# Loading the relative destinations and attribute rows of a graph network four chunks at a time

## The chip, the cores and the metric

The kernel runs on one core of a Trainium2 chip. The metric is the device time of one execution in microseconds. Before the change it is 8192.53 us, the median of three runs (8170.84, 8192.53, 8251.86). The engines are named as the profile names them: PE (TensorE; PEld is its weight load), DVE (VectorE), ACT (ScalarE), POOL (GpSimd) and SP (SyncE, which here only issues transfers).

## What is computed

A graph with 6,250 nodes of 128 features and 200,000 edges sorted by destination goes through two message-passing convolutions and one attention layer. Only the part that runs over the edges matters here. Cut to it, the reference is:

```python
def mesh_conv(x, src, dst, ea, w1, b1, g, bt, w2, b2):
    m = jnp.concatenate([x[dst], x[src], ea], axis=-1) @ w1 + b1
    m = jax.nn.silu(group_norm(m, g, bt))
    m = m @ w2 + b2
    out = jax.ops.segment_sum(m, dst, num_segments=n)
    cnt = jax.ops.segment_sum(jnp.ones((dst.shape[0],), m.dtype), dst, num_segments=n)
    return out / jnp.clip(cnt, 1.0)[:, None]
...
logits = (q[dst] * k[src]).sum(-1) * scale + (edge_attr @ ew + eb)
amax = jax.ops.segment_max(logits, dst, num_segments=n)
pe = jnp.exp(logits - amax[dst])
ssum = jax.ops.segment_sum(pe, dst, num_segments=n)
w = pe / jnp.clip(ssum[dst], 1e-06)
o = jax.ops.segment_sum(w[:, :, None] * v[src], dst, num_segments=n)
```

## The kernel before

The edges are cut into 196 chunks (`NCH`) of 1,024 edges (`CH`): 8 tiles (`NT`) of 128. Three stages run over all chunks, one after another: the first convolution, the second, and attention. Between them stand short node stages, which project all nodes and write tables to memory: `a_d` (the part of x[dst] @ w1, three bf16 pieces of a row of 128) and `b_d` (the part of x[src] @ w1) for the convolutions, `a_d` and `kv_d` for attention.

A chunk's destinations lie in a window of 112 (`WN`) rows of the table, because the edges are sorted. So x[dst] is not gathered: a one-hot matrix picks the rows by matmul. `rel_d` holds each edge's destination relative to its chunk's window, one row of 128 for each tile. `loads` (L442) does for one chunk: it spreads the chunk's 1,024 relative destinations over 112 partitions with one transfer into the tile `rel_b` (L447, 224 KB); it loads 16 (`KE`) rows of attributes and constants into partitions 112 to 127 of the tile `ohT` (L450, 32 KB); it loads the window's 112 table rows into one of three fixed tiles `pk` (L453, 84 KB); and on DVE it compares `rel_b` with the partition's number, which gives the one-hot matrix in partitions 0 to 111 of `ohT` (L454). The tile `ohT` is then the stationary side of 24 matmuls with `pk` (L578 in the convolutions, L740 in attention, where L746 uses it once more), which give the edge's destination part and its attribute part in one product.

`gather` (L457) fetches the source part: 8 indirect transfers from POOL for each chunk (L459), into one of 13 tiles `g` in a convolution, 11 in attention. In a convolution DVE adds the two parts (L590), ACT squares them (L592), DVE reduces the squares (L593). After a group of 8 chunks (`G`) ACT takes the square root of the group's variances; then each chunk gets its normalisation on DVE (L604, L607, L608), silu on ACT (L609), a one-hot matrix of its edges' destinations in the 128-row window on DVE (L465), its segment sum by 8 matmuls (L614), two masked copies on ACT (L648) and the addition into the table on DVE (L639). Attention has the same shape: products with the keys (L752), their reduction (L754), a segmented maximum for each group of 8 with rows `nbs` and `nbe` loaded from SP (L786), then weights and sums (L828).

`pipeline` (L524) sets the program order: in turn it starts chunk n+1 (`ahead`: loads, gather, products), does the first step of chunk n, and the second step of one or two chunks of the group before. The framework's scheduler moves instructions within each engine's queue somewhat from there; each engine then works its queue strictly in order, and so does SP with its transfers. Tiles come from pools with a fixed number of buffers: a tile is written again only when all that used its earlier content have finished. `rel` has 3 buffers in a convolution and 2 in attention, `ohT` has 3, `pk` are 3 tiles, and the PSUM tile `m` of the products has 2. So the transfers and the comparison for chunk c wait for the matmuls of chunk c-3.

Of the kernel before, what the change touches and what calls it, by code (L numbers as in the profile page):

```python
# [9 lines left out]
BF = mybir.dt.bfloat16  # L10
I32 = mybir.dt.int32
AF = mybir.ActivationFunctionType
ALU = mybir.AluOpType
# [6 lines left out]
P = 128  # L20
# [3 lines left out]
NT = 8  # L24
CH = NT * P
G = 8
WN = 112
KE = P - WN
PITCH = D + 4
# [8 lines left out]
def kernel(ctx: ExitStack, tc: tile.TileContext, x, src, dst, eat, w, out):  # L38
# [10 lines left out]
    nc = tc.nc  # L49
    N = x.shape[0]  # L50
    EW = src.shape[1]
    NCH = EW // NT
# [18 lines left out]
    iota_p = const.tile([P, 1], FP, name="iota_p")  # L71
# [39 lines left out]
    with tc.tile_pool(name="wprep", bufs=2) as wp:  # L111
# [18 lines left out]
        for i in (1, 2):  # L130
            t = const.tile([P, 2 * D], FP, name=f"wab_{i}")
# [4 lines left out]
            t = wp.tile([5, D], FP, name="wcb")  # L136
# [4 lines left out]
        t = wp.tile([5, H], FP, name="web")  # L141
# [24 lines left out]
    nc.vector.memset(web3, 0.0)  # L166
    nc.sync.dma_start(out=web3[WN:P, :], in_=web3_d)

# [14 lines left out]
    rel_d = dram.tile([EW, P], BF, name="rel_d")  # L183
    nbs_d = dram.tile([EW, P], BF, name="nbs_d")
    nbe_d = dram.tile([EW, P], BF, name="nbe_d")
    ea_d = dram.tile([KE, E], BF, name="ea_d")
    with tc.tile_pool(name="prep", bufs=1) as pp, tc.tile_pool(name="rows", bufs=2) as rp, \
            tc.tile_pool(name="prep_ps", bufs=2, space=PSUM) as pps:
        def by_chunk(t):
            return t.rearrange("p (c t) -> p c t", t=NT)  # L190
# [53 lines left out]
        rel = pp.tile([P, EW], FP, name="rel")  # L244
# [3 lines left out]
        nc.vector.scalar_tensor_tensor(  # L248
            by_chunk(main), by_chunk(rel), float(WN), good[:, :, None].to_broadcast([P, NCH, NT]),
            ALU.is_lt, ALU.mult)  # L250
# [66 lines left out]
        for a in range(4):  # L317
            t = rp.tile([P, EW], FP, name="ea_f")
# [115 lines left out]
    def value(t, c, engine, top):  # L434
        return nc.values_load(t[0:1, c:c + 1] if isinstance(c, int) else t[0:1, bass.ds(c, 1)],
                              engines=[engine], min_val=0, max_val=top,
                              skip_runtime_bounds_check_because=WHY)

    class Chunk:
        pass  # L440

    def loads(c, pools, rows_d):  # L442
        k = Chunk()
        k.c = c
        k.src, k.dm = src_i[:, c * NT:(c + 1) * NT], dm0[:, c * NT:(c + 1) * NT]
        k.rel = pools["rel"].tile([WN, CH], BF, name="rel_b")
        nc.sync.dma_start(  # L447
            out=k.rel, in_=rel_d[c * NT:(c + 1) * NT, :].rearrange("t p -> (t p)")[None, :].to_broadcast([WN, CH]))
        k.ohT = pools["ohT"].tile([P, CH], BF, name="ohT")
        nc.sync.dma_start(out=k.ohT[WN:P, :], in_=ea_d[:, c * CH:(c + 1) * CH])  # L450
        k.pk = pk[c % NPK]
        first = value(lo_i, c, SP, N - 1)
        nc.sync.dma_start(out=k.pk[:WN].rearrange("p s c -> p (s c)"), in_=rows_d[bass.ds(first, WN), :])  # L453
        nc.vector.tensor_scalar(k.ohT[:WN, :], k.rel, iota_p[:WN], None, ALU.is_equal)  # L454
        return k

    def gather(k, g, table_d):  # L457
# [56 lines left out]
    def spread(n):  # L514

        sizes = [G] * max(0, (n - 5) // G)
        rest = n - sum(sizes)
        while rest:
            s = min(max(rest // 2, 1), G)
            sizes.append(s)  # L520
# [26 lines left out]
    def conv(i):  # L547
# [3 lines left out]
        wide = D + 1 if i == 1 else D  # L551
        with ExitStack() as es:
            pool = lambda n, b, **kw: es.enter_context(tc.tile_pool(name=f"{n}{i}", bufs=b, **kw))
            pools = {"rel": pool("rel", 3), "ohT": pool("ohT", 3), "oh": pool("oh", 3),
                     "ps": pool("ps", 1, space=PSUM), "left": pool("left", 1)}
            gp, wk, vp = pool("gp", 1), pool("wk", 2), pool("vp", 2)
            ps_ = pools["ps"]

            gs = [gp.tile([P, NT, PITCH], FP, name=f"g{j}") for j in range(G + 5)]
            if i == 1:  # L560
# [19 lines left out]
            def ahead(c):  # L580
                k = loads(c, pools, a3_d[i])
                k.g = gs[c % len(gs)]
                gather(k, k.g, b_d[i])
                hidden(k, [(k.ohT, k.pk)])
                return k

            def first(k, var, j):

                k.mt = k.g[:, :, :D]
                nc.vector.tensor_tensor(k.mt, k.m, k.mt, ALU.add)  # L590
                sq = wk.tile([P, NT, D], FP, name="sq")
                nc.scalar.activation(sq, k.mt, AF.Square)  # L592
                return lambda: nc.vector.tensor_reduce(  # L593
                    var[:, j * NT * H:(j + 1) * NT * H], sq.rearrange("p t (g c) -> p (t g) c", c=HD), AX.X, ALU.add)

            def deviations(n, var):
                sd = vp.tile([P, G * NT * H], FP, name="sd")
                nc.scalar.activation(sd[:, :n], var[:, :n], AF.Sqrt, bias=eps_t, scale=1.0 / HD)
                rs = ps_.tile([P, G * NT * H], FP, name="rs")
                nc.vector.reciprocal(rs[:, :n], sd[:, :n])  # L600
                return rs
# [17 lines left out]
            def first_step(k):  # L619
                for f in state["reduce"]:  # L620
                    f()
                if state["j"] == 0:
                    state["var"] = vp.tile([P, G * NT * H], FP, name="var")
                state["reduce"] = [first(k, state["var"], state["j"])]
# [47 lines left out]
    def after_conv(i, A):  # L672
# [15 lines left out]
        nc.scalar.activation(A[:, :NW, :], A[:, :NW, :], AF.Silu)  # L688

    conv(1)  # L690
    with tc.tile_pool(name="node1", bufs=1) as np_:
        A = np_.tile([P, NW + 1, D], FP, name="A")
        after_conv(1, A)
        nc.vector.tensor_tensor(A[:, :NW, :], A[:, :NW, :], temb[:, None, :].to_broadcast([P, NW, D]), ALU.add)
        make_ab(A, 2)
    conv(2)
    with tc.tile_pool(name="node2", bufs=1) as np_:
        A = np_.tile([P, NW + 1, D], FP, name="A")
# [24 lines left out]
        nc.sync.dma_start(out=t[WN:P].rearrange("p s c -> p (s c)"), in_=zeros_b[:KE, :])  # L723
    with ExitStack() as es:
        pool = lambda n, b, **kw: es.enter_context(tc.tile_pool(name=f"{n}a", bufs=b, **kw))
        pools = {"rel": pool("rel", 2), "ohT": pool("ohT", 3), "oh": pool("oh", 2),
                 "ps": pool("ps", 1, space=PSUM)}
        gp, wk = pool("gp", G + 3), pool("wk", 2)
        ps_ = pools["ps"]
# [30 lines left out]
        def ahead(c):  # L760
            k = loads(c, pools, a3_d[3])
            k.g = gp.tile([P, NT, KV], FP, name="g")
            gather(k, k.g, kv_d)
            k.qe = []
            products(k, k.ohT, k.pk)
            biases(k, k.ohT, web3)
            return k
# [232 lines left out]
```

## Time and profile before

| | |
|---|---|
| median of three runs | 8192.53 us (8170.84 to 8251.86) |
| the profiled execution | 8242.21 us, its span 8240.4 us |
| mean granted TensorE clock | 0.666 |
| DMA | 702.81 MB, mean 85 GB/s, 422,049 packets |
| queue of SP's and ACT's transfers q1 | 210,920 packets, 258.43 MB, 10.3% of 16 engines |
| POOL's gathers q0 | 175,616 packets, 417.77 MB, 18.7% of 16 engines |
| the comparison L454 | 588 times, 299.1 us busy, median 480 ns |
| the gathers L459 | 4,704 of 0.95 to 0.97 us |

The page of the profile shows one execution. Its first part is each engine's busy time; the second is the span in 40 slices, where the two convolutions fill slices 2 to 27 and attention the rest; a further part lists groups of instructions by line, with the time the engine sat idle before them and what ended that time. "issue" means that the engine waited for nothing that the profile shows, "remote" that a semaphore ended the wait and the profile can't name who set it. Times in the timelines are microseconds from the start of the span. The chain of waits that ended last covers only the last node stage in this trace, so the edge stages have to be read from the waits and the timelines.

### The profile page before, as it was taken

What the parts mean: (1) busy time and instruction counts of PE and PEld (TensorE: products, weight loads), DVE (VectorE), ACT (ScalarE), POOL (GpSimd) and SP (SyncE); (2) the same over time, 40 slices, a digit from 0 to 9 for tenths busy, and PEclk for the clock granted to TensorE, in tenths of its full rate; (3) what the DMA queues carried; (4) which work ended last, traced back from release to release, by engine and by line L of the source; (5) the groups of instructions that cost most, each with busy time, mean ns of one, the idle gap of its engine ahead of it and who ended that gap; (6) DMA issues with size and microseconds to landing.
All of it is one profiled execution on the core that took longest, in us unless ns stands there. A gap on an engine that the chain in (4) does not pass through costs nothing. (4 is left out here: it accounts for less than half of the span.)

```text
span 8240.4 us, 87011 instructions
## 1 busy us (share of the span) xinstructions
PE 3684.0 (45%) x26465; PEld 3255.2 (40%) x26466; DVE 5153.9 (63%) x7719; ACT 1631.0 (20%) x3110; POOL 4542.3 (55%) x4723
## 2 busy tenths in 40 slices
PE   2144444444444414444444444442555555555553
PEld 1133343334334313433334433332444545544542
DVE  5266666666666726666666666683666666666666
ACT  2122222222222312222222222230000000000001
POOL 2556566666565056656656665504666666666650
PEclk9566666666666656666666666676676666666666
DMA  5222222222222122222222222213444444444441
GB/s 160 63 70 71 69 74 73 71 72 73 68 70 65 43 61 73 70 68 72 72 70 71 73 73 69 65 71 111 118 120 120 120 120 120 120 120 118 120 110 48
DMA packets 422049, 702.81 MB, mean 85 GB/s; under 512 B 116780, under 2 KB 237444, under 8 KB 421060
## 3 DMA queue, kind: packets, MB, share of 16 engines
q0 software_dynamic: 175616, 417.77, 18.7%
q1 hardware_dynamic: 210920, 258.43, 10.3%
q10 hardware_dynamic: 35036, 20.95, 0.9%
q8 instruction: 215, 3.52, 0.2%
q14 instruction: 262, 2.15, 0.1%
HBM read 649.99 MB, written 46.67 MB: 85 GB/s over the span
## 5 line engine op out<-in xcount | busy, mean ns | idle before, releaser
L459 POOL DMA_INDIRECT g<-b_d,src_i x3136 | 2977.0, 949 | 2227.8 <-PE u L614 785.5
L459 POOL DMA_INDIRECT g<-kv_d,src_i x1568 | 1523.4, 972 | 1164.6 <-issue 418.7
L614 PE MATMUL u<-g,oh 128*128 128x129 f32 (+1 forms) x6272 | 1292.0, 380 | 1309.6 <-ACT g L609 659.9
L614 PEld LDWEIGHTS u<-g,oh 128*128 128x128 f32 x6272 | 1183.8, 286 | 1418.7 <-ACT g L609 710.8
L578 PE MATMUL m<-pk,ohT 128*128 128x128 bf16 x9408 | 894.5, 258 | 1609.9 <-issue 977.8
L578 PEld LDWEIGHTS <-ohT 128*128 128x128 bf16 x9408 | 744.8, 118 | 1742.4 <-issue 1170.7
L639 DVE TENSOR_TENSOR flat<-flat,u 128x258 f32 (+1 forms) x392 | 164.2, 419 | 1343.2 <-ACT u L648 1178.1
L828 PE MATMUL u<-g,oh 128*128 128x145 f32 x3136 | 785.8, 438 | 420.6 <-issue 361.7
L828 PEld LDWEIGHTS u<-g,oh 128*128 128x128 f32 x3136 | 723.7, 318 | 454.8 <-issue 391.0
L648 ACT ACTIVATE u<-u,mask 128x129 f32<-128x129 f32 (+1 forms) x784 | 266.5, 340 | 2152.5 <-remote 1250.7
L590 DVE TENSOR_TENSOR g<-m,g 128x1024 f32<-128x1024 f32 x392 | 476.2, 1215 | 290.8 <-remote 232.8
L740 PE MATMUL qe<-pk,ohT 128*128 128x128 bf16 x4704 | 439.1, 257 | 367.0 <-DVE g L752 226.3
L609 ACT ACTIVATE g<-g 128x1024 f32<-128x1024 f32 x392 | 414.1, 1056 | 925.8 <-DVE g L608 471.4
L592 ACT ACTIVATE sq<-g 128x1024 f32<-128x1024 f32 x392 | 414.3, 1057 | 718.6 <-DVE g L590 438.7
L740 PEld LDWEIGHTS <-ohT 128*128 128x128 bf16 x4704 | 382.4, 119 | 406.1 <-issue 204.2
L872 DVE SCALAR_TENSOR_TENSOR nm<-u,nm 128x2 f32<-128x2 f32 x196 | 31.2, 159 | 768.1 <-remote 467.6
L454 DVE TENSOR_SCALAR ohT<-rel_b,iota_p 112x1024 bf16<-112x1024 bf16 x588 | 299.1, 514 | 331.6 <-remote 313.4
L593 DVE TENSOR_REDUCE var<-sq 128x64 f32<-128x1024 f32 x392 | 473.8, 1209 | 15.5 <-ACT sq L592 13.7
L465 DVE TENSOR_TENSOR oh<-cps,dm 128x1024 f32<-128x1024 f32 x392 | 476.7, 1216 | 0.0
L607 DVE TENSOR_TENSOR g<-g,cps 128x1024 f32<-128x1024 f32 x392 | 475.1, 1212 | 1.8
L608 DVE TENSOR_TENSOR g<-g,cps 128x1024 f32<-128x1024 f32 x392 | 475.2, 1212 | 0.2
L604 DVE TENSOR_TENSOR g<-g,rs 128x1024 f32<-128x1024 f32 x392 | 473.8, 1209 | 0.1
(196 smaller groups left out, 3563.9 us busy)
## 6 DMA issues: line engine op xcount, KB each, us to landing
rel_b<-rel_d SPq DMA_DIRECT2D x588, 224.0 KB
g<-b_d,src_i POOLq DMA_INDIRECT x3136
pk<-a_d SPq DMA_DIRECT2D x588, 84.0 KB
g<-kv_d,src_i POOLq DMA_INDIRECT x1568
ohT<-ea_d SPq DMA_DIRECT2D x588, 32.0 KB
a_d<-a SPq DMA_DIRECT2D x48, 192.0 KB
kv_d<-kv ACTq DMA_DIRECT2D x49, 132.0 KB
h_d<-A SPq DMA_DIRECT2D x2, 3136.0 KB
```

The source lines that it names most:

```text
L459: nc.gpsimd.indirect_dma_start(out=g[:, t, :table_d.shape[1]], out_offset=None, in_=table_d, in_offset=bass.IndirectOffsetOnAxis(ap=k.src[ ...
L465: nc.vector.tensor_tensor(k.oh, iota[:, None, :].to_broadcast([P, NT, P]), k.dm[:, :, None].to_broadcast([P, NT, P]), ALU.is_equal)
L578: nc.tensor.matmul(k.m[:, t, :], lhsT=a, rhs=b, start=(j == 0), stop=(j == len(pairs) - 1))
L590: nc.vector.tensor_tensor(k.mt, k.m, k.mt, ALU.add)
L592: nc.scalar.activation(sq, k.mt, AF.Square)
L593: return lambda: nc.vector.tensor_reduce(var[:, j * NT * H:(j + 1) * NT * H], sq.rearrange("p t (g c) -> p (t g) c", c=HD), AX.X, ALU.add)
L604: nc.vector.tensor_tensor(k.mt.rearrange("p t (g c) -> p t g c", c=HD), k.mt.rearrange("p t (g c) -> p t g c", c=HD), k.rs.rearrange("p (t ...
L607: nc.vector.tensor_tensor(k.mt, k.mt, over_edges(gam), ALU.mult)
L608: nc.vector.tensor_tensor(k.mt, k.mt, over_edges(bet), ALU.add)
L614: nc.tensor.matmul(k.u[:, 0, :wide], lhsT=k.oh[:, t, :], rhs=k.g[:, t, :wide], start=(t == 0), stop=(t == NT - 1))
L740: nc.tensor.matmul(qe[:, t, :], lhsT=lhs[:, e], rhs=rhs[:, s, :], start=(s == 0), stop=(s == 2))
L828: nc.tensor.matmul(k.u[:, :wide], lhsT=k.oh[:, t, :], rhs=k.g[:, t, :wide], start=(t == 0), stop=(t == NT - 1))
```

## The change

The relative destinations and the attribute rows of four chunks (`LG`) are loaded by one transfer each, into a tile `ohT` that holds four chunks side by side. The relative destinations land in partitions 0 to 111 of it, where the one-hot matrix is to stand, and the comparison of each chunk writes over them in place. The pool `rel` is gone; `ohT` has 2 buffers of four chunks (before 3 of one). The first group is loaded with chunk 0, each further group two chunks before its first chunk is started. The rest of the kernel is as it was; its lines stand 12 further down from the middle of `loads` on.

```diff
+LG = 4
...
+    def load_group(c, pools):
+
+        n = min(LG, NCH - c)
+        t = pools["ohT"].tile([P, LG, CH], BF, name="ohT")
+        f = t.rearrange("p c e -> p (c e)")
+        nc.sync.dma_start(
+            out=f[:WN, :n * CH],
+            in_=rel_d[c * NT:(c + n) * NT, :].rearrange("t p -> (t p)")[None, :].to_broadcast([WN, n * CH]))
+        nc.sync.dma_start(out=f[WN:P, :n * CH], in_=ea_d[:, c * CH:(c + n) * CH])
+        pools[c // LG] = t
+
     def loads(c, pools, rows_d):
         k = Chunk()
         k.c = c
         k.src, k.dm = src_i[:, c * NT:(c + 1) * NT], dm0[:, c * NT:(c + 1) * NT]
-        k.rel = pools["rel"].tile([WN, CH], BF, name="rel_b")
-        nc.sync.dma_start(
-            out=k.rel, in_=rel_d[c * NT:(c + 1) * NT, :].rearrange("t p -> (t p)")[None, :].to_broadcast([WN, CH]))
-        k.ohT = pools["ohT"].tile([P, CH], BF, name="ohT")
-        nc.sync.dma_start(out=k.ohT[WN:P, :], in_=ea_d[:, c * CH:(c + 1) * CH])
+        if c == 0:
+            load_group(0, pools)
+        if c % LG == LG // 2 and c + LG // 2 < NCH:
+            load_group(c + LG // 2, pools)
+        k.ohT = pools[c // LG][:, c % LG, :]
         k.pk = pk[c % NPK]
         first = value(lo_i, c, SP, N - 1)
         nc.sync.dma_start(out=k.pk[:WN].rearrange("p s c -> p (s c)"), in_=rows_d[bass.ds(first, WN), :])
-        nc.vector.tensor_scalar(k.ohT[:WN, :], k.rel, iota_p[:WN], None, ALU.is_equal)
+        nc.vector.tensor_scalar(k.ohT[:WN, :], k.ohT[:WN, :], iota_p[:WN], None, ALU.is_equal)
         return k
...
-            pools = {"rel": pool("rel", 3), "ohT": pool("ohT", 3), "oh": pool("oh", 3),
+            pools = {"ohT": pool("ohT", 2), "oh": pool("oh", 3),
...
-        pools = {"rel": pool("rel", 2), "ohT": pool("ohT", 3), "oh": pool("oh", 2),
+        pools = {"ohT": pool("ohT", 2), "oh": pool("oh", 2),
```

## The prediction

> **What bounds the kernel now.** I read the page's first part (busy time of each engine), then its slices, then the table of windows by stage, the list of waits, and last the timeline of one stage's start.
>
> ```profile
> PE 3684.0 (45%) x26465; PEld 3255.2 (40%) x26466; DVE 5153.9 (63%) x7719; ACT 1631.0 (20%) x3110; POOL 4542.3 (55%) x4723
> ```
>
> No engine is full. A POOL gather of 0.95 us is followed by 0.30 us of its own issue time, so POOL needs 8 x 1.25 = 10.0 us for a chunk. In the columns of the table by stage (start and end, length, then each engine's busy time) the two convolutions and the attention pass look like this:
>
> ```profile
> 250.00:2500.00 2250.00, 947.21 (x6992) 839.02 (x6993) 1393.07 (x1411) 549.44 (x755) 1363.98 (x1437) 0.66 0.25 70
> 2720.00:5300.00 2580.00, 1089.87 (x7778) 961.04 (x7779) 1585.30 (x1629) 642.48 (x920) 1466.72 (x1546) 0.65 0.24 69
> 5600.00:8000.00 2400.00, 1263.91 (x9387) 1137.62 (x9388) 1499.37 (x3617) 185.13 (x949) 1501.80 (x1547) 0.66 0.43 118
> ```
>
> 196 chunks in about 2,500 us are 12.6 us a chunk: POOL's 10.0 us is the nearest floor, DVE works 8 us of it, DMA engines are a quarter to 43% busy. What fills the rest is waiting around the loop DVE, ACT, PE, ACT, DVE, and behind it POOL waiting for a gather buffer. The list of waits (engine, line, who released it: total, times, longest) says so:
>
> ```profile
> DVE flat L639 <- ACT u L648: 1178.1, 197, 18.7
> POOL g L459 <- PE u L614: 785.5, 288, 55.1
> DVE ohT L454 <- remote: 313.4, 8, 64.5
> DVE ohT L454 <- PE m L578: 11.9, 5, 6.3
> DVE ohT L454 <- DMA rel_b<-rel_d: 6.1, 6, 1.8
> ```
>
> The last three lines are the comparison that the change touches. Its load holds it for 6.1 us in the whole execution; so **the loads are not what the kernel waits for**. 313.4 us are eight waits only, on an event whose setter the profile can't name. They stand where a stage starts. DVE there:
>
> ```profile
> 226.01 0.48 DVE L454 TENSOR_SCALAR ohT<-rel_b,iota_p 112x1024 bf16<-112x1024 bf16 x1
> 227.22 1.22 DVE L593 TENSOR_REDUCE var<-sq 128x64 f32<-128x1024 f32 x1 [0.73 <-issue]
> 278.17 0.48 DVE L454 TENSOR_SCALAR ohT<-rel_b,iota_p 112x1024 bf16<-112x1024 bf16 x1 [49.73 <-remote]
> 278.57 1.22 DVE L590 TENSOR_TENSOR g<-m,g 128x1024 f32<-128x1024 f32 x1
> 280.91 1.22 DVE L593 TENSOR_REDUCE var<-sq 128x64 f32<-128x1024 f32 x1 [1.12 <-issue]
> 345.37 0.48 DVE L454 TENSOR_SCALAR ohT<-rel_b,iota_p 112x1024 bf16<-112x1024 bf16 x1 [63.24 <-remote]
> 345.77 1.22 DVE L590 TENSOR_TENSOR g<-m,g 128x1024 f32<-128x1024 f32 x1
> ```
>
> and PE in the same stretch:
>
> ```profile
> 226.16 2.74 PE L578 MATMUL m<-pk,ohT 128*128 128x128 bf16 x24 [7.45 <-issue]
> 279.89 2.72 PE L578 MATMUL m<-pk,ohT 128*128 128x128 bf16 x24 [50.99 <-issue]
> ```
>
> With three ohT tiles the comparison of chunk 5 must wait until the matmuls of chunk 2 have read theirs. Those were issued by 228.9; the comparison ran at 278.17. PE's completion reaches the others that late while POOL gathers without a pause (86.5 us busy of the 116 from 229 to 345, which with its 0.30 us gaps is all of it). The other starts do the same: 64.5 and 48.1 us in the second convolution, 55.2 us at 5702 in attention. Why completions are late I can't tell from the trace.
>
> **What the Trainium skill says.** *DMA: Bandwidth & Descriptors*, section Bandwidth, measures 1 MB from HBM to SBUF at 6.15 us (341 GB/s); no transfer of that size stands in this trace, and I use the figure as a price. The same page, Queues, rings and completion order, says that each DMA engine takes turns between queues packet by packet, so a large load does not shut out the gathers; the trace shows them side by side, but with loads of 224 KB only. *VectorE: DVE Perf Modes*, in its description of the modes, makes the rate depend on type, step, alignment and memory; the trace agrees in that all 588 comparisons have one form and a median of 480 ns for 1024 elements, over twice the rate of the fp32 products (1.21 us).
>
> **The change part by part.** I compared the order of the two built programs too; no time comes from it.
>
> *Transfers.* 588 relative rows and 588 attribute rows become 147 and 147: 882 issues of about 0.32 us less on SP, 282 us of SP time. No engine waits for SP's issue: 6.1 us above is all that the load ever costs DVE. Worth 0 to 6 us; I take 0. Bytes are equal (588 x 224 KB = 132 MB). Rows grow from 2 KB to 8 KB, so 588 x (112 + 16) = 75,264 packets become 18,816 if a row stays one packet, of 422,049. With DMA engines at most 43% busy this is hidden.
>
> *Comparison.* 588 before and after, same 112x1024 form, now in place. Nearest rows: L607 in place takes 1212 ns, L465 out of place 1216 ns. So 0. The bad end, if in place lost the packed rate: 1.21 - 0.48 = 0.73 us x 588 = 430 us of DVE time; the skill's conditions don't include a separate output, so I leave that end out.
>
> *Order.* POOL's gathers stand in the same order, 99% of PE's and 92% of DVE's instructions at the same place; from chunk 16 of a stage on, the comparison stands where it stood. In steady work nothing moves but SP's queue. A group's two loads stand before the pk load of chunk 4g-2 and wait for the matmuls of chunk 4g-5, the last readers of that buffer; pk of chunk 4g-2 waits for the same matmuls, so SP is held no longer. Behind it are that pk load and, in attention, the nbs and nbe rows. They queue behind 1 MB: about 6 us later. From a chunk's last L578 to the first L578 three chunks on, taken from the timeline for c = 4g-2, it is 17.6 us at the least in both convolutions, 30 us in attention (L740). The first comparison of a group stands 42.6 us or more behind the matmuls that free its buffer. Both cover 6 us: cost 0. Were that cover gone, m would be late by the rest, then u, then the sums of L639.
>
> *Waits taken away.* Only the first comparison of a group still waits for anything. In steady work this wait cost 11.9 us. At the starts, comparisons of chunks 0 to 7 now stand ahead of the first sum L590, and DVE is free to do the sum of chunk 1 at about 237, once its gather has landed, not at 278.57. That frees its PSUM tile, and PE can issue the matmuls of chunk 3 then, not at 279.89. But what is late next is the sum of chunk 2: it needs the same late completion, 278. Chunk 3 follows about 50 us later (49 us from issue to completion for chunk 2), near 327, and POOL's burst ends at 345 as before. At 345 the change is then about two chunks ahead: the sums of chunks 3 and 4 came 14 and 18 us after 345.8. So 16 us a start, 48 us for three.
>
> *Waits added.* The first comparison of a stage needs 1 MB, not 256 KB: 6 us against about 2 us, and DVE stands in front of the projection's subtractions meanwhile: +4 us x 3 = 12 us (0 to 20).
>
> *Sum.* -48 + 12 = -36 us on the profiled execution's 8242 us (8240.4 span and 1.8 around it), which is 0.6% above the median of 8192.5. On the median: 8156.
>
> **Rivals.** *A, the likeliest: nothing in steady work, a little at the starts*, 8156, own range 8105 to 8215.
>
> *B, the starts unlock.* If the completions are late because DVE and SP stand waiting, not because POOL is busy, chunks would follow the gathers at 10.0 us. The eighth sum would be done near 213 + 9 x 10 + 10 = 313, where the ninth (L590 of chunk 8) came at 379.7: 67 us a start, 200 us in all, 7990. Fewer packets may also ease whatever makes completions late in steady work (PE's L578 waits 977.8 us for nothing the profile shows); 5% of that is 49 us, and with it B runs from 8110 down to 7990. For it: DVE is blocked in order by a wait that disappears. Against it: sums need the same completions.
>
> *C, the 1 MB bursts delay the gathers* (slower). Place: attention, then the convolutions, 147 bursts. POOL holds a turn of eight gathers; its idle time at L459 is 2227.8 + 1164.6 us, less 0.30 x 4704 = 1411, so 1981 us or 3.4 us a chunk, 13.5 us in four chunks, against 6 us of burst. If the slack is in the wrong place and a third of each burst is lost: 147 x 2.0 = 300 us, 8490; it decides from 82 / 147 = 0.56 us lost a burst. For it: POOL is the nearest floor. Against it: the same bytes pass now, and ACT waits for gathers only 169 us.
>
> *That the change doesn't do what it says* is excluded by the built order: 147 pairs of loads, no wait but on the buffer.
>
> **Numbers.** A 0.46, B 0.32, C 0.22. About 1% (82 us) is what a measurement can tell from no change: the three runs before span 81 us. Within 1%: 0.46; faster by more: 0.32; slower by more: 0.22. The range takes A, B down to 7990 and C up to a quarter of its price, 8275; C's rest and a little of B stay outside.
>
> **What will show it.** Right, if the waits of the comparison (now L466) on unnamed events fall from 313.4 to under 100 us, the sums of chunks 3 and 4 in a stage come 10 to 20 us earlier after the start, the period from chunk 20 to 190 stays within 1% of 12.6 us, and the comparison's median stays near 480 ns. B, if the ninth sum comes 50 us or more earlier. C, if POOL or ACT waits for gathers grow, or PE waits for pk. Wrong altogether, if the steady period moves by itself.

## The result, and the profile after

The kernel after the change takes 8193.41 us (median of 20 runs, 8166.65 to 8241.96); the kernel before, run beside it, 8183.70 us (20 runs, 8146.63 to 8251.86). The ratio is 1.0017, with a 95% interval of 1.0000 to 1.0034: no difference that matters, and if any, a loss of up to 28 us. The forecast was 8156, 36 us less than before.

The profiled execution spans 8206.8 us. The first part of its page, busy time of each engine, is that of before within 1%:

```profile
PE 3654.0 (45%) x26465; PEld 3249.2 (40%) x26466; DVE 5150.0 (63%) x7719; ACT 1631.6 (20%) x3110; POOL 4536.9 (55%) x4723
```

The table by stage (start and end, length, then busy time of PE, PEld, DVE, ACT, POOL, the granted clock, the share of the DMA engines and GB/s) for the same three stretches also shows the same picture. POOL does 1,357 us in the first stretch where it did 1,364, and 1,514 us in attention where it did 1,502:

```profile
250.00:2500.00 2250.00, 948.15 (x6944) 842.07 (x6943) 1381.82 (x1398) 545.68 (x750) 1357.35 (x1432) 0.65 0.27 70
2720.00:5300.00 2580.00, 1083.49 (x7811) 961.83 (x7808) 1591.08 (x1636) 646.00 (x925) 1468.42 (x1550) 0.65 0.27 69
5600.00:8000.00 2400.00, 1259.24 (x9501) 1144.01 (x9501) 1518.69 (x3672) 189.38 (x970) 1513.60 (x1559) 0.67 0.45 119
```

What did change is the list of waits (engine, line, releaser: total us, times, longest):

```profile
DVE flat L651 <- ACT u L660: 1148.2, 206, 17.1
...
DVE g L602 <- remote: 468.6, 27, 63.6
...
DVE ohT L466 <- DMA ohT<-rel_d: 22.3, 10, 4.6
```

The sum's own line before the change was

```profile
DVE g L590 <- remote: 232.8, 23, 14.9
```

The comparison (L466) no longer waits for any unnamed event; its 313.4 us are gone, and what is left is 22.3 us for the larger loads. But the sum (L602) now waits 468.6 us where it waited 232.8. Together the two waited 546 us for unnamed events before, and wait 469 us after: **most of the wait moved from the comparison to the sum behind it**. (In two further profiles of the kernel after the change, taken with the experiments, the sum waits 569.2 and 375.5 us and the comparison none.) In the start of stage 1, the timeline of DVE shows it (start, length, instruction; in brackets the idle time before it and what ended it):

```profile
237.17 1.22 DVE L602 TENSOR_TENSOR g<-m,g 128x1024 f32<-128x1024 f32 x1 [6.49 <-DMA g<-b_d,src_i]
...
267.52 1.23 DVE L602 TENSOR_TENSOR g<-m,g 128x1024 f32<-128x1024 f32 x1 [26.78 <-remote]
...
334.72 1.23 DVE L602 TENSOR_TENSOR g<-m,g 128x1024 f32<-128x1024 f32 x1 [63.58 <-remote]
...
361.41 1.23 DVE L602 TENSOR_TENSOR g<-m,g 128x1024 f32<-128x1024 f32 x1 [18.05 <-remote]
...
376.98 1.21 DVE L602 TENSOR_TENSOR g<-m,g 128x1024 f32<-128x1024 f32 x1
```

These are the sums of chunks 1 to 4 and, last, 8. The fourth and the ninth of before were

```profile
359.91 1.22 DVE L590 TENSOR_TENSOR g<-m,g 128x1024 f32<-128x1024 f32 x1
...
379.66 1.22 DVE L590 TENSOR_TENSOR g<-m,g 128x1024 f32<-128x1024 f32 x1
```

The second sum, that of chunk 1, stands at 237.17, as forecast (278.57 before). The third waits for the late completion of chunk 2's matmuls, the fourth, at 334.72, for that of chunk 3's. From 361 on the sums follow one another, and the ninth, at 376.98, has gained 2.7 us. The PE timeline of the same stretch shows the last matmul of chunk 3, then those of chunk 4 and the first ones of chunk 5:

```profile
247.90 0.26 PE L590 MATMUL m<-pk,ohT 128*128 128x128 bf16 x1 [2.54 <-issue]
268.79 1.01 PE L590 MATMUL m<-pk,ohT 128*128 128x128 bf16 x8 [20.63 <-issue]
273.80 0.26 PE L590 MATMUL m<-pk,ohT 128*128 128x128 bf16 x1 [4.00 <-issue]
...
313.70 0.26 PE L590 MATMUL m<-pk,ohT 128*128 128x128 bf16 x1 [2.54 <-issue]
335.99 1.01 PE L590 MATMUL m<-pk,ohT 128*128 128x128 bf16 x8 [22.03 <-issue]
```

PE is late in two ways. Chunk 4's 24 matmuls of 0.26 us take from 268.79 to 313.96, with 2.54 us before each of the later ones in which PE waits for nothing that the profile shows. And completions arrive late: the last matmul of chunk 3 stands at 247.90, the sum that reads its result at 334.72. POOL's burst of 13 chunks of gathers ends at 345.4; after it PE's gaps shrink, and from 361 on its matmuls follow one another again. The removed wait stood in front of this, not in place of it.

One fact must be known before the experiments are read. The kernels of one measurement ran on one chip, beside the kernel before, and each of the five further measurements on a different chip. In three measurements, that of the result among them, the kernel before takes 8181 to 8293 us; in the three others it takes 6751 us, and no engine waits for an unnamed event at all in any profile taken there (none of them is of the kernel before itself). I call them chips with late and with timely completions. No chip was measured twice, so that the chip makes the difference, and not something else that changed between the measurements, is likely but not shown. Ratios are always to the kernel before on the same chip.

### The profile page after: what moved, and what is told of

Same layout as the page of the kernel before. It is cut to its first block, busy times and chain, and to the rows that moved or that the text cites. A ratio compares the mean times of both kernels' runs of the same rounds, so it can differ in the third digit from the quotient of the medians.

```text
span 8206.8 us, 85701 instructions
## 1 busy us (share of the span) xinstructions
PE 3654.0 (45%) x26465; PEld 3249.2 (40%) x26466; DVE 5150.0 (63%) x7719; ACT 1631.6 (20%) x3110; POOL 4536.9 (55%) x4723
## 2 busy tenths in 40 slices
DMA packets 351479, 702.67 MB, mean 86 GB/s; under 512 B 102668, under 2 KB 223332, under 8 KB 331684
## 5 line engine op out<-in xcount | busy, mean ns | idle before, releaser
L602 DVE TENSOR_TENSOR g<-m,g 128x1024 f32<-128x1024 f32 x392 | 476.0, 1214 | 535.0 <-remote 468.6
L764 DVE TENSOR_TENSOR g<-qe,g 128x512 f32<-128x512 f32 x392 | 265.9, 678 | 136.0 <-remote 86.3
```

## The experiments

**One chunk a load, eight buffers** (timely chip). The wait on the buffer is taken away without the large transfers (attention gets 8 buffers too):

```diff
-LG = 4
+LG = 1
...
-        if c == 0:
-            load_group(0, pools)
-        if c % LG == LG // 2 and c + LG // 2 < NCH:
-            load_group(c + LG // 2, pools)
+        load_group(c, pools)
...
-            pools = {"ohT": pool("ohT", 2), "oh": pool("oh", 3),
+            pools = {"ohT": pool("ohT", 8), "oh": pool("oh", 3),
```

> The comparison in place as after the change, but every chunk is loaded by itself (256 KB with its attribute rows), into 8 buffers of one chunk, which is the same memory. So the wait on the buffer is taken away and the size of the transfers stays that of before. My theory (the wait taken away only moves to the sum, which needs the same late matmuls): the comparison's waits on unnamed events fall from 313 us to under 30, the sum's rise to about 470, the ninth sum of stage 1 stands within 10 us of 377, and the time is 0.995 to 1.003 of before; the first load of a stage is short again, so up to 6 us a start less than after the change. Rival, the size of the transfers matters (fewer packets help, or the bursts cost something that hides a gain): the ratio lies 0.6% or more (49 us) away from that of after the change, in the one direction or the other.

**One chunk a load, three buffers** (the same chip): as above, with 3 in place of 8, so the comparison in place alone.

> The comparison in place alone: single chunks, 3 buffers as before, the rows loaded straight into the tile that the matmuls read. A load now waits for the matmuls of three chunks earlier, where before only the comparison did. My theory: the comparison's waits stay (250 to 380 us, now put down to the load where that came last), its median stays 480 ns, the loads are covered in steady work, ratio 0.997 to 1.004 of before. Rival, the load behind the matmuls has no cover: 2 us or more for a good part of 588 chunks, the comparison waits over 200 us longer and the kernel is slower by over 1%.

Measured: 6760.77 us, ratio 1.0014 (1.0008 to 1.0021), with eight buffers; 6753.43, ratio 1.0003 (0.9995 to 1.0011), with three. With three buffers the comparison waits 4.7 us for its loads and nothing else of note, and its median is 479 ns: the comparison in place costs nothing, and neither does a load that waits for the matmuls. But the waits that I had expected there, 250 to 380 us, don't exist on this chip, so half of both expectations was void. The table by stage of the kernel with three buffers, in stretches inside its two convolutions and attention, says what holds it:

```profile
250.00:2100.00 1850.00, 921.37 (x7272) 855.24 (x7272) 1456.57 (x1474) 571.01 (x792) 1400.43 (x1476) 0.72 0.31 88
...
4600.00:6500.00 1900.00, 1144.23 (x9136) 1048.23 (x9133) 1458.34 (x3554) 183.19 (x940) 1441.00 (x1478) 0.73 0.52 143
```

1,476 gathers of 1.25 us are 1,845 of 1,850 us: POOL is full, and the sums of chunks 20 to 190 follow one another at 10.02 us, the floor that I had worked out, where the late chips take 12.3 to 12.9 us in the convolutions. DVE's timeline at the start of stage 1 is that of rival B, with the waits on gathers alone:

```profile
241.53 1.23 DVE L599 TENSOR_TENSOR g<-m,g 128x1024 f32<-128x1024 f32 x1 [6.28 <-DMA g<-b_d,src_i]
...
242.68 0.48 DVE L463 TENSOR_SCALAR ohT<-ohT,iota_p 112x1024 bf16<-112x1024 bf16 x1
...
251.51 1.22 DVE L599 TENSOR_TENSOR g<-m,g 128x1024 f32<-128x1024 f32 x1 [6.36 <-DMA g<-b_d,src_i]
```

The sums (L599 here) of chunks 2 and 3 stand one gather period apart, and so do all up to the ninth, at 301.4. Three buffers are enough for it: where completions are timely, the wait that the change removes isn't there. Eight buffers give nothing more; with them the kernel takes 7 us longer.

**Each group's 1 MB loaded twice in the convolutions** (the same chip), the second time into a tile that nobody reads. With `twice` in a convolution's pools, `load_group` ends:

```diff
+        if "twice" in pools:
+            h = pools["twice"].tile([P, LG * CH], BF, name="twice")
+            nc.sync.dma_start(
+                out=h[:WN, :n * CH],
+                in_=rel_d[c * NT:(c + n) * NT, :].rearrange("t p -> (t p)")[None, :].to_broadcast([WN, n * CH]))
+            nc.sync.dma_start(out=h[WN:P, :n * CH], in_=ea_d[:, c * CH:(c + n) * CH])
```

> As after the change, but in the two convolutions each group's 1 MB is loaded a second time, into a tile that nobody reads: 98 further bursts of 1 MB on the same queue, right behind the first. My theory: loads of that size cost nothing in steady work, 0 to 25 us (only the two first groups of a stage, 6 us each, stand on a path): ratio to after the change 0.998 to 1.004. Rival, bursts delay the gathers or the rows of pk behind them: 0.56 to 2.0 us a burst, 55 to 196 us slower than after the change, with more time in which PE waits for pk or the sum for a gather.

Measured: 6774.30 us, ratio 1.0035 (1.0023 to 1.0047). The kernel after the change itself had no run on a timely chip; the held-back kernel below is the same but for 20 small copies for which nobody waited there, and it took 6766.65 and 6767.30 us (1.0023, 1.0014 to 1.0032, both times). These ran on other timely chips, beside a kernel before of the same 6751 us. So 98 further bursts cost about 7 us, 0.07 us each, against the 0.56 at which rival C begins to decide. The stretch 300 to 2100 of the table by stage, first for the doubled loads:

```profile
300.00:2100.00 1800.00, 918.44 (x7145) 853.43 (x7143) 1435.98 (x1452) 562.97 (x784) 1362.54 (x1435) 0.71 0.44 114
```

and for the held-back kernel, with the loads once:

```profile
300.00:2100.00 1800.00, 928.83 (x7158) 864.84 (x7155) 1436.94 (x1452) 564.79 (x785) 1362.83 (x1441) 0.71 0.33 87
```

The DMA engines are busy 44% of the stretch instead of 33% and move 114 GB/s instead of 87, and POOL, which is full, does its 1,363 us of gathers in both. C is out in the convolutions, on the chip where POOL had no slack to hide it. In attention, which rival C named first, nothing was doubled, but there too the gathers of chunks 20 to 190 follow one another at 10.24 us a chunk both with loads of one chunk (three and eight buffers) and with loads of four (the held-back kernel, first run).

**Ten gather tiles instead of thirteen** (the same chip), `range(G + 2)` for `range(G + 5)` in `conv`.

> As after the change, with 10 gather tiles in a convolution instead of 13, so POOL's first burst of a stage is 10 chunks long, not 13: it should pause at about 315 us instead of 345. My theory (PE's completions come late as long as POOL gathers without a pause): PE's slow stretch in stage 1, one matmul in about 2.5 us, ends near 315, about 30 us earlier, and the ninth sum comes near 350 instead of 377; in steady work POOL waits for buffers sooner, which costs 0 to 1.5 us a chunk in the convolutions, so the whole is 0 to 600 us slower. Rival (PE is late for a reason of its own at the start of a stage, for instance its clock, or the other loads): the slow stretch ends near 345 as before.

Measured: 7104.31 us, ratio 1.0527 (1.0510 to 1.0543). Completions were timely, so the question, when PE's slow stretch ends, has no answer here. What it shows is the worth of the three tiles: the convolutions' period is 10.91 us instead of 10.01, and 0.90 us for 392 chunks are 353 us, against the 337 us by which this kernel is above the held-back one below.

**The kernel after the change again, and the first chunk loaded by itself** (both on a late chip). The second one loads a stage's first group in two parts:

```diff
+        for o, w in ([(0, 1), (1, n - 1)] if c == 0 else [(0, n)]):
+            at = slice(o * CH, (o + w) * CH)
```

with both transfers of `load_group` inside the loop, over the columns `at`.

> The kernel after the change once more, beside the kernel before on the same chip. On the chip of the last four kernels the program before takes 6751 us, not 8184, its matmuls' completions come in time and POOL's gathers follow one another at 10.0 us a chunk. My theory: where completions come in time, the change has no wait to take away; what is left is the first load of each stage, 1 MB in place of 256 KB, 2 to 6 us each: ratio 1.001 to 1.003, and the first gather of stage 1 stands 2 to 6 us later than the 209.6 us of the kernel with single chunks and 3 buffers. Rival: the wait taken away does gain where completions are on time, ratio under 0.999. If the chip is one where completions are late, both unnamed waits and the ratio are as in the first measurement, 1.0017.

> As after the change, but the first group of a stage is loaded in two parts: chunk 0 alone (256 KB with its attribute rows), then chunks 1 to 3. My theory: the price of the change is that first load, so the first gather of each stage stands 2 to 6 us earlier than after the change, and the kernel is 6 to 15 us faster than it (0.1 to 0.2%): ratio to before 0.999 to 1.001. Rival (the price lies elsewhere, in the order of DVE's comparisons or in steady work): no more than 3 us between this kernel and the one after the change.

Measured: 8345.27 us, ratio 1.0050 (1.0027 to 1.0074), for the change; 8329.54, ratio 1.0045 (1.0022 to 1.0068), with the first chunk alone. The first gather of stage 1 stands at 211.4 instead of 217.7, 6.4 us earlier, so the edit does what it should; in the whole its 16 us can't be told from nothing.

**Plain transfers, or fills, in place of the first gathers.** Both were meant to tell what in POOL's burst makes PE late.

```diff
-                gather(k, k.g, b_d[i])
+                if c < len(gs):
+                    for t in range(NT):
+                        w = (c * NT + t) % NW
+                        nc.scalar.dma_start(out=k.g[:, t, :D], in_=b_d[i][w * P:(w + 1) * P, :])
+                else:
+                    gather(k, k.g, b_d[i])
```

> As after the change, but the gathers of the first 13 chunks of each convolution are left out; in their place ACT issues 8 plain transfers of 64 KB a chunk, of fixed rows of the same table into the same tiles (so the sums of these chunks are of other rows). The same bytes move, but POOL does nothing in the start of a stage. Where completions are late (a chip on which the kernel before takes over 8000 us): my theory, it is POOL's gathering without a pause that makes PE's completions late, so here the start of a convolution runs freely: unnamed waits of the sum under 100 us instead of 469 to 569, and the ninth sum within 60 us of the first one instead of 150 to 158. Rival 1, it is the traffic of the transfers: the ninth sum comes over 100 us after the first. Rival 2, it is PE itself after an idle node stage: the same.

In the other, `nc.gpsimd.memset(k.g[:, :, :D], 0.125 * (t + 1))` stands for the transfer.

> As after the change, but POOL's gathers of the first 13 chunks of each convolution are replaced by 8 fills of the gather tile a chunk, done by POOL itself (so the sums of these chunks take a constant for the gathered rows). POOL is as busy as with gathers, but issues no transfers. Where completions are late: if POOL's being busy alone is enough, PE's slow stretch stays as long as the fills last and ends with them; if it takes the issue of gathers (or their traffic), which is what I expect, the ninth sum comes within 30 us of the end of the ninth chunk's fills and the sum's unnamed waits are under 100 us.

Measured: 6651.52 us, ratio 0.9849 (0.9831 to 0.9867), and 6709.75, ratio 0.9935 (0.9917 to 0.9953). The chip was a timely one, so both are silent on the question. They leave gathers out, so they aren't versions to use; the 115 us that the first is under the held-back kernel on that chip say only what the two bursts cost where POOL is the bound.

**POOL held back at the start of a convolution** (timely chips, twice).

```diff
+            pace = vp.tile([1, 1], FP, name="pace")
...
+                if 3 <= c < len(gs):
+                    nc.gpsimd.tensor_copy(pace, gs[c - 3][0:1, 0, 0:1])
                 gather(k, k.g, b_d[i])
```

> As after the change, with POOL held back at the start of a convolution: before the gather of chunk c, for c from 3 to 12, POOL copies one number of the tile of chunk c-3, which it can do only when the sum of that chunk is done. So POOL can't run on for 13 chunks while PE's completions are late. Where completions are late: my theory, POOL pauses after the third chunk, PE's completions then arrive at once and the start follows the gathers: the ninth sum at 320 to 350 instead of 377, 25 to 55 us less for each of the two convolutions, 50 to 110 us in all, ratio 0.990 to 0.998 of before. Rival (PE is late whether POOL gathers or not): POOL only loses its lead, the ninth sum comes at 370 or later and the kernel is 0 to 60 us slower than after the change. Where completions are in time, nobody waits for the copy: within 5 us of after the change.

> The kernel with POOL held back by a copy before the gathers of chunks 3 to 12 once more: on the chip of its first run completions were in time (before 6751 us), nobody waited for the copy, and nothing could be told. If completions are late this time (before over 8000 us): my theory as then, POOL pauses, PE's completions arrive, the ninth sum of stage 1 comes at 320 to 350 instead of 377, and the kernel is 50 to 110 us faster than after the change, whose ratio was 1.0017 and 1.005. Rival, PE is late whether POOL gathers or not: the ninth sum at 370 or later, 0 to 60 us slower than after the change. If they are in time again: 1.002 as in the first run.

Measured: ratio 1.0023 both times, as said above; POOL waited for none of the copies. It served as a stand-in for the kernel after the change.

**Held back, and the first chunk alone; the kernel after the change beside it** (a late chip). The two edits above in one kernel.

> Both small edits in one: the first group of a stage loaded in two parts (chunk 0 alone, then chunks 1 to 3), and POOL held back by the copy before the gathers of chunks 3 to 12. Where completions are in time (before near 6751 us) only the first edit can do anything. My theory, the price of the change is that first load: 2 to 6 us a stage less than after the change, ratio to before 0.9995 to 1.0015, and the first gather of stage 1 at 209 to 213 us instead of 216 to 217. Rival, the price lies elsewhere: within 3 us of the kernel after the change. Where completions are late (before over 8000 us): POOL pauses, PE's completions arrive, the ninth sum of stage 1 is at 320 to 350 instead of 372 and the kernel 50 to 110 us faster than the one with the first group in two parts alone (ratio 1.0045); or, if PE is late whether POOL gathers or not, the ninth sum at 370 or later and no gain.

> The kernel after the change once more, on the chip of the kernel before this. Where completions are in time: no wait of the comparison to take away, POOL's gathers at 10.0 us a chunk set the time, so the change costs what the first loads cost: ratio 1.001 to 1.003, within 0.1% of the two runs of the held-back kernel (1.0023 twice). Rival: its steady period, too, differs from the 10.02 us of the kernels with single chunks, ratio over 1.004 or under 0.999. Where completions are late: 1.0017 to 1.005 as in the two earlier measurements.

Measured: 8132.95 us, ratio 0.9938 (0.9914 to 0.9962), against 8213.69, ratio 1.0055 (1.0032 to 1.0077), for the kernel after the change: 81 us less, and faster than both kernels. The waits of POOL's copies are 27.3 us in all, four of the twenty copies. The two of stage 1 in POOL's timeline:

```profile
263.75 0.94 POOL L473 DMA_INDIRECT g<-b_d,src_i  x1 [0.30 <-issue]
271.60 0.18 POOL L599 COPY pace<-g 1x1 f32<-1x1 f32 x1 [6.90 <-DVE g L607]
272.26 0.98 POOL L473 DMA_INDIRECT g<-b_d,src_i  x1 [0.48 <-issue]
...
318.61 0.18 POOL L599 COPY pace<-g 1x1 f32<-1x1 f32 x1 [6.33 <-DVE g L607]
```

PE at the same time:

```profile
252.03 0.26 PE L593 MATMUL m<-pk,ohT 128*128 128x128 bf16 x1 [1.83 <-issue]
271.52 2.72 PE L593 MATMUL m<-pk,ohT 128*128 128x128 bf16 x24 [19.23 <-DVE g L607]
275.04 2.72 PE L593 MATMUL m<-pk,ohT 128*128 128x128 bf16 x24 [0.80 <-DVE g L607]
```

and DVE:

```profile
270.24 1.23 DVE L607 TENSOR_TENSOR g<-m,g 128x1024 f32<-128x1024 f32 x1 [30.19 <-remote]
...
273.77 1.21 DVE L607 TENSOR_TENSOR g<-m,g 128x1024 f32<-128x1024 f32 x1
...
326.96 1.21 DVE L607 TENSOR_TENSOR g<-m,g 128x1024 f32<-128x1024 f32 x1
```

The fourth and the ninth sum of the kernel beside it, without the copies:

```profile
333.45 1.23 DVE L602 TENSOR_TENSOR g<-m,g 128x1024 f32<-128x1024 f32 x1 [63.58 <-remote]
...
378.04 1.22 DVE L602 TENSOR_TENSOR g<-m,g 128x1024 f32<-128x1024 f32 x1
```

Up to 252 PE goes as slowly as in the kernel after the change. POOL's last gather before the copy ends at 264.69; some 5.5 us later the third sum runs, and then the fourth at 273.77 instead of 333.45. PE issues its 24 matmuls in 2.72 us again. Once POOL has gathered for some 15 us more, PE is late once more, until the next pause, from 312 on. In all four pauses, two in each convolution, the awaited sum runs 5.0 to 6.4 us after POOL's last gather. The ninth sum stands at 327.0 against 378.0. So on this late chip **PE's completions are held up while POOL gathers without a pause, and a pause of 6 to 8 us frees them**: the rival, that PE is late anyway, is out.

Counted from the first gather, 49 us are gained at the ninth sum of stage 1 (112.4 against 161.8) and 58 in stage 2 (112.2 against 170.1). The first chunk alone doesn't do this: in its run without the copies, above, the ninth sums stand 161.1 and 168.4 us after the first gather. At the 21st sum 26 and 32 us of the gain are left; those 58 us are most of the 81 us between the medians. The two profiled executions are 102 us apart. In them chunks 20 to 190 take 8 us more in the first convolution than in the kernel beside it and 48 us less in the second (periods of 12.43 and 12.31 us against 12.38 and 12.59), which I can't tell from scatter.

## Why the prediction was right, and where it wasn't

Its likeliest case, no change to be seen, came true; its time, -36 us, has the wrong sign: +14 us, 0 to 28, and +41 and +45 us in the two further measurements on late chips. It came true because every term of its sum is small beside the 82 us of 1%, not because its largest term was understood.

*Transfers, comparison, order: 0.* These held. The comparison in place keeps 480 ns as its median, as the conditions that the Trainium skill states in *VectorE: DVE Perf Modes* had suggested. Loads of 1 MB behind each other cost 0.07 us each where POOL is full. PE waited 27.1 us for `pk` after the change, 24.6 before, and ACT in the convolutions 166.8 us for gathers, 169.2 before. The convolutions' period from chunk 20 to 190 is 12.61 and 12.49 us, 12.55 and 12.54 before. Packets fell by more than forecast, from 422,049 to 351,479: about 18,800 more of 8 KB or larger, as forecast, and besides 14,112 fewer under 512 B, which are 16 for each of the 882 transfers saved.

*Waits taken away: -48 us. This is the step that failed*, and in it the words "At 345 the change is then about two chunks ahead ... So 16 us a start". The wait did vanish, and the ones that I named as next in line, sums 2 and 3, took its place. But PE issued most of chunk 4's matmuls only every 2.1 to 2.8 us, up to 314, where I had let completions follow every 50 us. So when the burst ended at 345, the change was one chunk ahead, not two: the sum of chunk 3 was done where before that of chunk 2 just ran. And a lead of one chunk is then worth one step of the sums that follow, (377.0 - 361.4) / 4 = 3.9 us, not the 14 to 18 us by which the sums of chunks 3 and 4 had stood behind that of chunk 2. From the first gather to the ninth sum it is 166.5 us before and 161.6 after in stage 1, 171.7 and 169.4 in stage 2; in attention the gathers of chunk 20 start 269.1 and 270.4 us after those of chunk 0. That is 7 us gained in the convolutions and 1 lost in attention: 6 us for the starts, not 48. (The two further profiles of the kernel after the change, on other chips, have 160.9 and 161.8, 170.0 and 170.1, 274.3 and 273.3 us, which leaves 2 us.) My sign "the sums of chunks 3 and 4 in a stage come 10 to 20 us earlier" was off the same way: 25 and 2 us in stage 1.

*Waits added: +12 us.* The size is right, though made otherwise. In the tile's view, the load and the comparison of the kernel after the change first start at (last pair of times in each line: first and last start)

```profile
L466 DVE TENSOR_SCALAR ohT<-ohT,iota_p x588: 467/480/695, 192.2 to 8037.7; 112x1024 bf16<-112x1024 bf16 x196
L448 SPq DMA_DIRECT2D ohT<-rel_d x147: 308/316/551, 186.2 to 7930.4; - x147
```

and in the kernel with single chunks and three buffers at

```profile
L448 SPq DMA_DIRECT2D ohT<-rel_d x588: 303/311/626, 186.6 to 6536.4; - x196
...
L463 DVE TENSOR_SCALAR ohT<-ohT,iota_p x588: 467/479/711, 189.9 to 6586.2; 112x1024 bf16<-112x1024 bf16 x196
```

6.0 us and 3.3 us. The first is near the 6.15 us that the Trainium skill's *DMA: Bandwidth & Descriptors* gives for 1 MB (Bandwidth), though that figure is only the busy time of the DMA engines and this one runs from the issue of 896 KB to their reader. The step is 2.7 us rather than 4. The rest I put down to the eight comparisons, not three, that stand among DVE's work for the tables: on timely chips the first gather of stage 1 comes at 209.6 with single chunks and three buffers, at 213.7 with single chunks and eight, where eight comparisons stand there too, and at 216.2 in the held-back kernel. The whole costs 13 to 14 us there (6766.65 and 6767.30 against 6753.43).

*The sum* is then -6 + 14 = +8 us, inside the measured 0 to 28. It is an estimate, since the 14 us were measured on timely chips alone. The further 34 to 38 us of the two later measurements I can't place: no profile of the kernel before stands beside them, and three single profiles of the kernel after the change differ by up to 0.56 us a chunk in the convolutions' steady period (12.38 to 12.94).

*Rivals.* B, that the starts unlock, didn't happen by the change; its schedule is real where completions are timely (ninth sum at 301.4, I had estimated 313), and the pauses of POOL reach two thirds of it (327 between 378 and 301). That completions are not late because DVE stands at the comparison is shown by the kernel after the change, where it no longer does and they still are; that POOL's unbroken gathering holds them up is shown by the held-back kernel. C is excluded by the doubled loads and the period in attention. Two slips of the working don't bear on the outcome: a quarter of C's 300 us on 8192.5 is 8267, not 8275, and B's "eighth sum" at 313 is the ninth, that of chunk 8.

*Open:* why some chips are late and others not; whether POOL's being busy is enough, or it takes its issuing of gathers, or the traffic that they start (the two kernels for it ran on a timely chip); what holds the steady period on late chips at 12.3 to 12.9 us, which is most of their distance from the others (2.5 us for 392 chunks are 980 of some 1,430 us); and whether pauses in steady work would pay there, which wasn't tried.

## What to carry to other kernels

Before you price a wait, ask what the instruction behind it needs: here the comparison and the sum after it needed the same late matmuls, and the first one's 313 us of waits went, the second one's grew by 236, and the starts of the stages gained 6. When an engine's completions come late, look for the one whose unbroken run goes with it, and test it by making that one pause; here 27 us of pauses went with 81 us less. And measure on more than one chip: the same program took 6751 us or 8181 to 8293 us, with another bound.

## What was not expected of the hardware

The kernel before takes 6751.4, 6751.3 and 6751.6 us on three chips and 8184, 8293 and 8181 us in the measurements on late ones. Its mean granted clock is 0.72 (median of its executions) on the former and 0.66 to 0.67 on the latter. That doesn't account for 1,430 us: PE is busy 3,654 us in the kernel after the change on a late chip and 3,484 in the held-back kernel on a timely one, 170 us less.

At a stage's start on the late chips, while POOL gathers without a pause, PE issues most matmuls of 0.26 us, ready as far as the profile shows, one every 2.1 to 2.8 us, and DVE waits for its completions, up to 64.5 us in one piece (second convolution of the kernel before). Where POOL paused for a copy, they were there 5.0 to 6.4 us after its last gather. On the other chips the same gathers, 1.25 us apart, leave PE undisturbed: in the kernel with three buffers every chunk's 24 matmuls at the start of stage 1 take 2.7 us.
